# A cross-attention and Strassen feed-forward kernel: the first keys on another queue, the first normalisation reordered, and small work moved between units

## The chip, the cores and the metric

One core of a Trainium2 chip runs the whole program. The metric is the device time of one execution in microseconds; lower is better. The engines are TensorE (PE, with its weight loads PEld), VectorE (DVE), ScalarE (ACT), GpSimd (POOL) and SyncE (SP), which only issues transfers. ScalarE and GpSimd issue transfers too. Each engine runs its own instructions strictly in the order in which the program emitted them.

## The reference

The input is `x` (8 x 256 x 256), a context of the same shape and a key mask. Each row of `x` is normalised over its 256 values and attends, causally, to the context, which is keys and values at once; the result is added to `x`. The sum is normalised again and goes through a feed-forward network with ternary weights, each with a scale for every output; its result is added once more:

```
x = x + softmax(mask(layernorm(x) @ ctx.T / 16)) @ ctx
y = layernorm(x)
h = silu((y @ w1.T) * s1) * ((y @ w2.T) * s2)     # 256 -> 1024
h = gelu((h @ h1.T) * t1)                         # 1024 -> 1024
h = gelu((h @ h2.T) * t2)                         # 1024 -> 1024
out = x + (h @ w3.T) * s3                         # 1024 -> 256
```

## The kernel before, in words

The 2048 tokens are four blocks `t` = 0 to 3 of 512 tokens (two batches `j`). The blocks run in two pairs `s`: pair 0 holds blocks 0 and 1, pair 1 blocks 2 and 3. A pair's two blocks go through the two 1024 x 1024 products together, as a Strassen scheme with seven products of halves of 512; a block's hidden values are in halves `a` and `b` (first block) and `c` and `d` (second block), and sums such as `T1 = c - a` and `T2 = d - T1` are operands. Every operand is split into a rounded part `oh` (a cast on ScalarE, `parted`) and a rest `ol` (a subtraction on VectorE, `rest`, L313), and both are multiplied.

**Units and the plan.** `pair(s, ...)` is a generator; what it emits between two `yield`s is a unit, and each pair has 80. Units 0 to 7 are the gated first layer of the pair's first block (`pa`, `pb`, then SiLU `gate` on ScalarE L697 and a product with it on VectorE L700). For the first hidden layer follow: product 1 (8 to 11), product 2, called `second`, whose four results `p` are added to `na` by VectorE L855 (12 to 15), the gated layer of the second block with the making of T1 and T2 (16 to 23), and products 6, 5, 3, 7, 4 (24 to 43). The second hidden layer runs products 1, 6, 5, 3, 7, `second`, 4 (44 to 71), and units 72 to 79 are the output layer (`po`, `res` L711). Most units take TensorE 1.81 us. After each unit the actions that the table `plan` names for it are emitted, so the numbers in `stages_at`, `looks` and `at` decide where in each engine's queue the small work stands.

**Stages.** The attention of a block (`stages`) is a chain of such actions. For blocks 2 and 3 the queries come from memory; late in the chain `sums` takes the statistics of the new `x`, `on_all` turns mean and reciprocal deviation over (TensorE `tmf` L393, a copy, and a path through memory), L659 and L660 normalise on VectorE and GpSimd, `casts` (ScalarE L606) and `rests` (VectorE L313) make `hyt` and `lyt`, the operands of the gated layer, and the transfer `kept` stores the transposed `x` for the end.

**Head.** Block 0 is split into two groups, one batch each, that advance in turn stage by stage, so that each engine has the other group's work between two steps of one. For each group: `sums` (L261, L262), `normed` (square root L269 on ScalarE, reciprocal L275, `scaled` L283 on VectorE, giving `ya`), `turned` (TensorE `pqt`), a scaled copy to `qt`, scores `ps`, softmax, `pv`, the add to `x` (L551), and the second normalisation. Group 0's second normalisation is taken by ScalarE from sums, and its finish (`begun`) lies in the list `held`, from which `sums` of group 1 takes it. Five warm-up matmuls stand on TensorE's queue between `pxt` and `pyt` of group 1. All loads of block 0 but the mask are issued by SP: four tiles of `x`, then the keys `kt` of group 0 and of group 1, then `vs`.

**Looks.** `look_through` tests 22 pieces of the weights in turn: six small ones, each with one VectorE reduce (`seen`, L212), and 16 wide ones, each with a sign pass on ScalarE (L216) and a comparing pass on VectorE (L218). One call issues the load of piece k (`raw`, 512 KB, three buffers, on SP), finishes with L218 the piece signed by the call before, and signs or reduces piece k - 2. A call's load waits for the buffer that its own L218 frees. Twenty-five calls are needed.

Of the kernel before, what the change touches and what calls it, by code (L numbers as in the profile page):

```python
# [43 lines left out]
P = 128  # L44
B, S, D, H = 8, 256, 256, 1024
NB = 2
NT = NB * S // P
# [27 lines left out]
def _network(ctx, tc, g, exact, flag):  # L75
# [23 lines left out]
    def groups(t):  # L99

        return ((0,), (1,)) if t == 0 else ((0, 1),)
# [4 lines left out]
    def tiles(js):  # L106
        return slice(2 * js[0], 2 * js[-1] + 2)

    def load_block(t, behind=None):

        xs = new(io, [P, NT, D], "xs", f"xs_{t}", bufs=2)
        kt = new(io, [P, NB, ND, S], "kt", f"kt_{t}", bufs=2)
        vs = new(io, [P, NT, D], "vs", f"vs_{t}", bufs=2)
        mi = new(io, [P if t else 1, TB], "mi", f"mi_{t}", I32)
        span = bass.ts(t, TB)
        if behind is not None:
            for tile_ in (xs[:, 0, :1], kt[:, 0, 0, :1], vs[:, 0, :1], mi[:, :1]):
                behind.memset(tile_, 0)
        if t == 0:
            nc.scalar.dma_start(out=mi, in_=g.mask[:, span])  # L120
        step = NT if t else 1
        for i in range(0, NT, step):
            nc.sync.dma_start(out=xs[:, i : i + step, :], in_=g.x[t, :, i : i + step, :])
        for n, js in enumerate(groups(t)):
            own = slice(js[0], js[-1] + 1)
            nc.sync.dma_start(out=kt[:, own], in_=g.ctx_t[t, :, own])
            if n == 0 and t:
                nc.sync.dma_start(out=mi, in_=g.mask[:, span].to_broadcast([P, TB]))
        nc.sync.dma_start(out=vs, in_=g.ctx_n[t])
        return xs, kt, vs, mi  # L130
# [123 lines left out]
        yield  # L254
        yield nc.values_load(flag[0:1, 0:1], min_val=0, max_val=P * (LOW + len(wide) * RAW))

    def sums(src, js, mv, name, between=()):

        stats = new(tiny, [P, NT, nc.vector.BN_STATS_DIM], "stats", f"st{name}", bufs=2)
        for i in range(NT)[tiles(js)]:  # L260
            nc.vector.bn_stats(out=stats[:, i, :], in_=src[:, i, :])  # L261
            nc.vector.bn_aggr(out=mv[:, :, i], in_=stats[:, i, :])  # L262
            while between:
                between.pop()()

    def root(js, mv, name):
        own = tiles(js)
# [10 lines left out]
    def normed(src, js, mv, y, name):  # L278
        scaled(src, range(NT)[tiles(js)], mv, turned_over(js, root(js, mv, name), name), y)
# [32 lines left out]
    def rest(lo, value, hi):  # L312
        nc.vector.tensor_tensor(lo, value, hi.bitcast(F32), ALU.subtract)  # L313
# [91 lines left out]
    def queries_turned(t, js, once, xs, mi, pss):  # L405

        cols = tokens(js)
        mva = once("mva", "mva", [P, nc.vector.BN_AGGR_DIM, NT], tiny, bufs=2)
        sums(xs, js, mva, f"a_{t}_{js[0]}")
        if t == 0 and js == groups(t)[0]:  # L410
            nc.vector.tensor_scalar(row16[:, :TB], mi, 0.0, NEG, ALU.is_equal, ALU.mult)
        if not t:
            masks_first(js, pss)
        yield
        y = once("y", "ya", [P, NT, D])
        normed(xs, js, mva, y, f"a_{t}_{js[0]}")
        if t == 0 and js == groups(t)[-1]:
            passed = new(const, [P, 1], "passed", "passed")
            nc.gpsimd.tensor_copy(passed, y[:, NT - 1, :1])
        yield  # L420
        bias = mask_bias(t, js, once, mi)
        qt = once("qt", "qt", [P, ND, TB])
        for c, pt in turned(y, js, f"pqt_{t}_{js[0]}", *(() if t else (ps_mm, "mm"))):

            if t or js == groups(t)[0]:
                nc.scalar.activation(qt[:, c, cols], pt, AF.Copy, scale=1.0 / 16.0)
            else:
                nc.vector.tensor_scalar(qt[:, c, cols], pt, 1.0 / 16.0, None, ALU.mult)
        table(t, js, AF.Exp)
        yield  # L430
        return qt, bias, None
# [25 lines left out]
    def stages(t, js, once, result, xs, kt, vs, mi):  # L457
# [68 lines left out]
        for j in js:  # L526
            if t:
                pv = ps_at.tile([P, 2, D], F32, tag="at", name=f"{v}pv_{t}_{j}")
                pvs = [pv[:, h, :] for h in range(2)]
            else:  # L530

                p, tag = (ps_at, "at") if j else (ps_mm, "mm")
                pvs = [p.tile([P, D], F32, tag=tag, name=f"{v}pv_0_{j}_{h}") for h in range(2)]
            for h, (a, e) in enumerate(SPANS):
                n = (e - a) // P
                for k in range(n):
                    nc.tensor.matmul(  # L537
                        pvs[h],
                        lhsT=prt[:, j, bass.ds(a + k * P, P)],
                        rhs=vs[:, 2 * j + k, :],  # L540
                        start=(k == 0),
                        stop=(k == n - 1),
                    )

            first_ = len(groups(t)) > 1 and js == groups(t)[0]
            if first_:
                total, centre, squares, std = (
                    new(const, [P, 2], n, n) for n in ("total", "centre", "squares", "std0")
                )
            for h in range(2):  # L550
                nc.vector.scalar_tensor_tensor(  # L551
                    xs[:, 2 * j + h, :],
                    pvs[h],
                    rden[:, j, h : h + 1],
                    xs[:, 2 * j + h, :],
                    ALU.mult,
                    ALU.add,
                    **(dict(accum_out=total[:, h : h + 1]) if first_ else {}),
                )
        if t:  # L560
            yield
        mvf = once("mvf", "mvf", [P, nc.vector.BN_AGGR_DIM, NT], tiny)
        if first_:
            y = once("y", "yf", [P, NT, D])
            for i in range(2):
                nc.scalar.activation(
                    centre[:, i : i + 1], total[:, i : i + 1], AF.Copy, scale=-1.0 / D
                )
                nc.scalar.activation(
                    y[:, i, :],  # L570
                    xs[:, i, :],
                    AF.Square,
                    bias=centre[:, i : i + 1],
                    accum_out=squares[:, i : i + 1],
                )
            nc.scalar.activation(std, squares, AF.Sqrt, bias=eps, scale=1.0 / D)

            def begun():

                nc.vector.reciprocal(std, std)  # L580
                shifted(0, nc.gpsimd)

            def shifted(i, engine):
                engine.tensor_scalar(
                    y[:, i, :],
                    xs[:, i, :],
                    centre[:, i : i + 1],
                    std[:, i : i + 1],
                    ALU.add,
                    ALU.mult,  # L590
                )

            held.append(begun)
        else:
            sums(xs, js, mvf, f"f_{t}_{js[0]}", held)
        yield
        xst = once("xst", "xst", [P, ND, TB])
        yt = []
# [13 lines left out]
        def rests(values):  # L612
            for c, value in values if not exact else ():
                rest(yt[1][:, c, cols], value, yt[0][:, c, cols])

        def turned_x():
            pxt = turned(xs, js, f"pxt_{t}_{js[0]}")
# [8 lines left out]
        if near(t):  # L626
# [16 lines left out]
            if not t and not first_:  # L643
                residual_turned(pxt)
            yield
            rests(values)
        else:
            std = once("sq", "sdf", [P, NT], tiny, bufs=2)
            nc.scalar.activation(std, mvf[:, 1, :], AF.Sqrt, bias=eps)
# [12 lines left out]
            values = [(slice(c, c + 1), y[:, c : c + 1, :]) for c in range(ND)]  # L662
            casts(values)
            yield
            rests(values)
        if js == groups(t)[-1]:
            nc.sync.dma_start(out=kept(t), in_=xst)
        result[:] = yt
# [124 lines left out]
    def half(tag, name):  # L793

        return new(hp, [P, 2, TB], tag, name, bufs=2)
# [37 lines left out]
    def pair(s, places, stock):  # L833
# [74 lines left out]
        for n in (2, 3):  # L908
# [64 lines left out]
            if first_:  # L973
# [4 lines left out]
                for o in range(NH):  # L978
# [10 lines left out]
                    )  # L989
                    if not s and o in (2, 4):  # L990
                        fetch(o // 2 + 1)
                    if o in (2, 4):
                        T1[o // 2 - 1] = half(place["T1"], f"T1_{name}_{o}")
                        sub(T1[o // 2 - 1], c[o // 2 - 1], a[o // 2 - 1])

                    if o == 5:
                        T2[:] = [half(place["T2"], f"T2_{name}_{h}") for h in range(2)]
                        sub(T2[0], d[0], T1[0])
                    if o == 6:
                        X[6] = parted(T2[:1], f"{name}_6")  # L1000
                        rest(X[6][0][1], T2[0], X[6][0][0])
                        sub(T2[1][:, 0, :], d[1][:, 0, :], T1[1][:, 0, :])
# [165 lines left out]
    def sums_from(r):  # L1168
# [5 lines left out]

    stages_at(1, (0, 0), (0, (1, 2, 4, 5, 7, 9, 10, 10, 10, 11, 13, 14)))
    stages_at(
        2, (0, 8), (0, (25, 28, 30, 41, 45, 46, 49, 51, 53, 54, 55, 57, 58, 61, 62, 63))
    )
    stages_at(
        3, (0, 30), (0, (55, 56, 59, 70, 73, 74, 75, 77, 78, 79)), (1, (0, 1, 5, 8, 10, 13))  # L1180
    )
    at(0, (7, 7, 14, 15), lambda: next(summing[2], None))
    at(0, 9, lambda: sums_from(0))
# [1 line left out]
    at(0, 21, lambda: sums_from(1))  # L1185
    at(0, (32, 33, 34, 37), lambda: next(summing[4], None))
    at(0, 44, lambda: w3.extend(load_weight(g.w3t, "w3_")))
    at(0, (72, 74, 76, 78), lambda: next(looking, None))
    looks = (1, 3, 5, 8, 10, 12, 14, 16, 17, 19, 26, 27, 42, 44, 46, 47, 50, 51, 54, 55, 58)
    at(1, looks, lambda: next(looking, None))  # L1190
    at(1, 61, lambda: [None for _ in looking])
    at(1, (66, 70), lambda: next(ending))
# [65 lines left out]
```

## Time and profile before

| | us |
|---|---|
| median of three runs | 349.14 |
| lowest and highest | 347.75, 349.73 |
| the profiled execution, its own time | 347.43 |
| its span, first to last instruction | 345.6 |
| TensorE, VectorE, ScalarE, GpSimd busy | 334.0, 270.3, 216.4, 36.6 |

The clock that TensorE was granted was 0.995 of full speed. Times in the lines below are microseconds from the start of the span. A line of the timeline gives start, time, engine, source line, operation, output and inputs, their shapes and the number of instructions, and in brackets how long the engine had been idle and what ended that. A matmul's end is modelled and overlaps the next one, so lost time is read from the starts.

### The profile page before, as it was taken

The numbers are of one execution on the slowest core, as the hardware profiler recorded it, in microseconds if no ns is written. First come the engines' busy times: TensorE is split into PE (matmuls) and PEld (weight loads), VectorE is DVE, ScalarE is ACT, GpSimd is POOL, SyncE is SP. The second block draws the span as 40 slices with busy tenths as digits, with TensorE's granted clock in tenths as the row PEclk, the third lists the DMA queues.
The fourth block names the chain that finished last, engine by engine and source line by source line (L and its number), as shares of the span: only waits on it lengthen the run. The fifth ranks groups of instructions, "written<-read, shape, count | busy, mean of one in ns | idle before, by whom it ended". The sixth has DMA issues, their size and how long they took to land.

```text
span 345.6 us, 4329 instructions
## 1 busy us (share of the span) xinstructions
PE 334.0 (97%) x1508; PEld 269.9 (78%) x1508; DVE 270.3 (78%) x411; ACT 216.4 (63%) x301; POOL 36.6 (11%) x78
## 2 busy tenths in 40 slices
PE   8999999999999999999999999999999999999991
PEld 4777887877888888887888788886788887888781
DVE  5779876999799848686997875889948987856761
ACT  4866833358855854858671675356896686767620
POOL 3610000210002300030000003000010000000000
PEclk9999999999999999999999999999999999999998
DMA  5999972997596642579517474960635579530032
GB/s 184 342 297 273 294 256 82 358 280 252 151 399 228 197 146 99 164 251 326 204 47 246 127 251 127 292 248 2 243 123 182 173 250 353 201 121 0 0 123 70
DMA packets 20702, 68.81 MB, mean 199 GB/s; under 512 B 2465, under 2 KB 5313, under 8 KB 17090
## 3 DMA queue, kind: packets, MB, share of 16 engines
q0 software_dynamic: 7488, 36.70, 33.0%
q1 hardware_dynamic: 13040, 31.63, 27.2%
q8 instruction: 14, 0.23, 0.3%
q14 instruction: 14, 0.11, 0.1%
q10 hardware_dynamic: 146, 0.13, 0.1%
HBM read 55.86 MB, written 8.40 MB: 186 GB/s over the span
## 4 chain that ended last, share of the span: by engine, by line
PE 79%; DVE 8%; DMA 5%; ACT 3%; issue 2%; POOL 1%; DVEq 0%; POOLq 0%; ACTq 0%; SPq 0%
PE px_u L824 29%; PE px_y L824 15%; PE po L1112 8%; PE p L824 7%; PE pa L684 5%; PE pb L684 5%; PE ps L470 3%; PE pv L537 3%; DMA raw<-h2q 3%; DMA raw<-h1q 1%; DVE sign L218 1%; DVE ol L313 1%; PE pqt L301 1%; ACT oh L807 1%; DVE sta L261 1%
## 5 line engine op out<-in xcount | busy, mean ns | idle before, releaser
L824 PE MATMUL px_u<-oh,a 128*128 128x512 f32 x256 | 71.7, 395 | 1.1 <-ACT oh L807 0.8
L824 PE MATMUL px_u<-ol,a 128*128 128x512 f32 x256 | 70.8, 391 | 0.0
L824 PEld LDWEIGHTS px_u<-ol,a 128*128 128x128 f32 x256 | 47.9, 188 | 11.6 <-DVE ol L313 1.5
L824 PEld LDWEIGHTS px_u<-oh,a 128*128 128x128 f32 x256 | 47.5, 188 | 11.8 <-ACT oh L807 1.2
L697 ACT ACTIVATE gate<-pa,sc 128x512 f32<-128x512 f32 x32 | 21.6, 686 | 24.5 <-PE pa L684 22.1
L824 PE MATMUL px_y<-oh,a 128*128 128x512 f32 x128 | 34.5, 391 | 0.0
L824 PE MATMUL px_y<-ol,a 128*128 128x512 f32 x128 | 34.2, 389 | 0.0
L824 PEld LDWEIGHTS px_y<-ol,a 128*128 128x128 f32 x128 | 24.0, 188 | 5.0
L824 PEld LDWEIGHTS px_y<-oh,a 128*128 128x128 f32 x128 | 23.9, 188 | 5.0
L216 ACT ACTIVATE sign<-raw 128x1024 bf16<-128x1024 f32 x16 | 16.9, 1055 | 9.5 <-DMA raw<-h2q 4.1
L768 POOL DMA_DIRECT2D a<-S x16 | 8.5, 534 | 131.6 <-PE px_u L824 55.5
L218 DVE SCALAR_TENSOR_TENSOR sign<-raw,sign 128x1024 bf16<-128x1024 f32 x16 | 19.3, 1219 | 2.7 <-ACT sign L216 2.7
L684 PE MATMUL pa<-hyt,w 128*128 128x512 f32 x60 | 19.1, 399 | 0.2 <-DVE na L855 0.2
L684 PE MATMUL pb<-hyt,w 128*128 128x512 f32 x60 | 18.6, 391 | 0.2 <-DVE res L711 0.2
L684 PE MATMUL pa<-lyt,w 128*128 128x512 f32 x60 | 18.5, 390 | 0.0
L684 PE MATMUL pb<-lyt,w 128*128 128x512 f32 x60 | 18.5, 389 | 0.0
L852 ACT ACTIVATE nd<-nd,sc 128x512 f32<-128x512 f32 x16 | 10.7, 715 | 11.7 <-DVE nd L855 11.7
L824 PE MATMUL p<-oh,a 128*128 128x512 f32 x64 | 17.4, 394 | 0.4 <-DVE na L855 0.4
L313 DVE TENSOR_TENSOR ol<-nT,oh 128x1024 fp32r<-128x1024 f32 x12 | 14.5, 1222 | 3.6 <-ACT oh L807 3.6
L824 PE MATMUL p<-ol,a 128*128 128x512 f32 x64 | 17.1, 389 | 0.0
L855 DVE TENSOR_TENSOR na<-p,na 128x512 f32<-128x512 f32 x16 | 10.9, 688 | 7.9 <-PE p L824 7.9
L852 ACT ACTIVATE nb<-nb,sc 128x512 f32<-128x512 f32 x16 | 10.7, 717 | 10.0 <-DVE nb L855 10.0
(196 smaller groups left out, 651.1 us busy)
## 6 DMA issues: line engine op xcount, KB each, us to landing
a<-S POOLq DMA_DIRECT2D x16, 1024.0 KB, 5.1
a<-h1q POOLq DMA_DIRECT2D x6, 1024.0 KB, 7.8
a<-h2q POOLq DMA_DIRECT2D x6, 1024.0 KB, 5.1
raw<-h1q SPq DMA_DIRECT2D x8, 512.0 KB, 4.3
raw<-h2q SPq DMA_DIRECT2D x8, 512.0 KB, 5.9
vs<-ctx_n SPq DMA_DIRECT2D x4, 512.0 KB, 7.5
q<-h1q POOLq DMA_DIRECT2D x4, 512.0 KB, 20.1
q<-h2q POOLq DMA_DIRECT2D x8, 256.0 KB, 14.0
```

Source lines behind the costliest of these rows:

```text
L216: nc.scalar.activation(sign, raw, AF.Sign)
L218: nc.vector.scalar_tensor_tensor(sign, raw, 1.0, sign, ALU.mult, ALU.not_equal, accum_out=count[:, n : n + 1])
L313: nc.vector.tensor_tensor(lo, value, hi.bitcast(F32), ALU.subtract)
L470: nc.tensor.matmul(pss[j][h], lhsT=qt[:, c, bass.ts(2 * j + h, P)], rhs=kt[:, j, c, : e - a], start=(c == 0 and t > 0), stop=(c == ND - 1) ...
L537: nc.tensor.matmul(pvs[h], lhsT=prt[:, j, bass.ds(a + k * P, P)], rhs=vs[:, 2 * j + k, :], start=(k == 0), stop=(k == n - 1),)
L684: nc.tensor.matmul(pm, lhsT=wc[:, bass.ts(o, P)], rhs=x, start=(n == 0), stop=(n == len(steps) - 1),)
L697: nc.scalar.activation(gate, pa, AF.Silu, scale=sc[:, 0, o : o + 1])
L768: nc.gpsimd.dma_start(out=a, in_=src)
L824: nc.tensor.matmul(bank, lhsT=a[:, k, bass.ts(o, P)], rhs=x[k // 2][part][:, k % 2, :], start=start and (part, k) == steps[0], stop=stop a ...
L852: nc.scalar.activation(out, src, AF.Gelu, scale=sc[:, n, o : o + 1])
L855: nc.vector.tensor_tensor(out, one, other, ALU.add)
L1112: nc.tensor.matmul(po, lhsT=w3[j * QK + k][:, bass.ts(o, P)], rhs=xs_[j][k // 2][part][:, k % 2, :], start=(j == 0 and (part, k) == STEPS[0]),
```

## The change

1. **Keys.** The first group's keys are issued on ScalarE's queue instead of SP's.
2. **First normalisation.** Group 0's square root, reciprocal and scaling (its tile 0 on GpSimd) are put into `held` and emitted between the two tiles of group 1's `sums`.
3. **Adds.** In block 0's group 1, `sums` emits each tile's add (L551) just ahead of that tile's statistics (`ahead`), and `held` is taken before the second tile instead of after the first.
4. **T1.** In pair 1 the second half of T1 is made in unit 21 behind T2's first half, instead of in unit 20.
5. **Block 2's rests** become three actions, in units 68, 69 and 69 (and with them `kept`), instead of one in unit 63. Block 3's are split the same way but stay in unit 13 of pair 1.
6. **Looks.** In pair 0 the four calls come two units earlier. In pair 1 the calls at 17 and 19 become one at 18, and those at 50 and 51 move to 51 and 52; the last call is made by the clearing action of unit 61.
7. **Statistics turned.** Block 3's `on_all` moves from unit 1 to unit 2 of pair 1.

```diff
-            nc.sync.dma_start(out=kt[:, own], in_=g.ctx_t[t, :, own])
+            queue = nc.sync if t or n else nc.scalar
+            queue.dma_start(out=kt[:, own], in_=g.ctx_t[t, :, own])
...
-    def sums(src, js, mv, name, between=()):
+    def sums(src, js, mv, name, between=(), ahead=None):
-        for i in range(NT)[tiles(js)]:
+        for n, i in enumerate(range(NT)[tiles(js)]):
+            if ahead is not None:
+                ahead(n)
+            while n and between:
+                between.pop()()
             nc.vector.bn_stats(out=stats[:, i, :], in_=src[:, i, :])
             nc.vector.bn_aggr(out=mv[:, :, i], in_=stats[:, i, :])
-            while between:
-                between.pop()()
...
-        sums(xs, js, mva, f"a_{t}_{js[0]}")
-        if t == 0 and js == groups(t)[0]:
+        sums(xs, js, mva, f"a_{t}_{js[0]}", held)
+        y = once("y", "ya", [P, NT, D])
+        very_first = t == 0 and js == groups(t)[0]
+        if very_first:
+            def begun():
+                rstd = turned_over(js, root(js, mva, "a_0_0"), "a_0_0")
+                scaled(xs, (0,), mva, rstd, y, nc.gpsimd)
+                scaled(xs, (1,), mva, rstd, y)
+            held.append(begun)
...
-        normed(xs, js, mva, y, f"a_{t}_{js[0]}")
+        if not very_first:
+            normed(xs, js, mva, y, f"a_{t}_{js[0]}")
...
-            for h in range(2):
+            def added(h, j=j, pvs=pvs):
...
+            if t or first_:
+                added(0)
+                added(1)
...
-            sums(xs, js, mvf, f"f_{t}_{js[0]}", held)
+            sums(xs, js, mvf, f"f_{t}_{js[0]}", held, None if t else added)
...
                 rest(yt[1][:, c, cols], value, yt[0][:, c, cols])
+                yield
...
-            rests(values)
+            yield from rests(values)
...
-                    if o in (2, 4):
-                        T1[o // 2 - 1] = half(place["T1"], f"T1_{name}_{o}")
-                        sub(T1[o // 2 - 1], c[o // 2 - 1], a[o // 2 - 1])
+                    if o == 2:
+                        T1[:] = [half(place["T1"], f"T1_{name}_{h}") for h in range(2)]
+                        sub(T1[0], c[0], a[0])
+                    if o == 4 and not s:
+                        sub(T1[1], c[1], a[1])
                     if o == 5:
                         T2[:] = [half(place["T2"], f"T2_{name}_{h}") for h in range(2)]
                         sub(T2[0], d[0], T1[0])
+                    if o == 5 and s:
+                        sub(T1[1], c[1], a[1])
...
-        2, (0, 8), (0, (25, 28, 30, 41, 45, 46, 49, 51, 53, 54, 55, 57, 58, 61, 62, 63))
+        2, (0, 8), (0, (25, 28, 30, 41, 45, 46, 49, 51, 53, 54, 55, 57, 58, 61, 62, 68, 69, 69))
...
-        3, (0, 30), (0, (55, 56, 59, 70, 73, 74, 75, 77, 78, 79)), (1, (0, 1, 5, 8, 10, 13))
+        3, (0, 30), (0, (55, 56, 59, 70, 73, 74, 75, 77, 78, 79)), (1, (0, 2, 5, 8, 10, 13, 13, 13))
...
-    at(0, (72, 74, 76, 78), lambda: next(looking, None))
-    looks = (1, 3, 5, 8, 10, 12, 14, 16, 17, 19, 26, 27, 42, 44, 46, 47, 50, 51, 54, 55, 58)
+    at(0, (70, 72, 74, 76), lambda: next(looking, None))
+    looks = (1, 3, 5, 8, 10, 12, 14, 16, 18, 26, 27, 42, 44, 46, 47, 51, 52, 54, 55, 58)
```

More of the change, by code (lines that the diff above doesn't have):

```diff
@@ L414, in queries_turned @@
         yield
-        y = once("y", "ya", [P, NT, D])
-        normed(xs, js, mva, y, f"a_{t}_{js[0]}")
+        if not very_first:
+            normed(xs, js, mva, y, f"a_{t}_{js[0]}")
         if t == 0 and js == groups(t)[-1]:
@@ L645, in stages @@
             yield
-            rests(values)
+            list(rests(values))
         else:
@@ L664, in stages @@
             yield
-            rests(values)
+            yield from rests(values)
         if js == groups(t)[-1]:
```

## The prediction

> **What bounds the kernel now.** I read the page's busy table first:
>
> ```profile
> PE 334.0 (97%) x1508; PEld 269.9 (78%) x1508; DVE 270.3 (78%) x411; ACT 216.4 (63%) x301; POOL 36.6 (11%) x78
> ```
>
> TensorE (PE) sets the time; nothing in the change touches its work, so only its waits and the head before its steady stream (from 18.69 us) count. Next I read TensorE's timeline for holes. Four 512-column matmuls start every 0.91 us, 0.227 each; whatever exceeds that is lost.
>
> ```profile
> 155.76 1.07 PE L824 MATMUL p<-ol,a 128*128 128x512 f32 x4
> 157.27 0.50 PE L824 MATMUL p<-oh,a 128*128 128x512 f32 x1 [0.43 <-DVE na L855]
> ...
> 191.02 0.61 PE L684 MATMUL pa<-lyt,w 128*128 128x512 f32 x2
> 191.83 0.73 PE L684 MATMUL pb<-hyt,w 128*128 128x512 f32 x2 [0.20 <-DVE res L711]
> 192.40 0.62 PE L684 MATMUL pb<-lyt,w 128*128 128x512 f32 x2
> 193.27 0.27 PE L393 MATMUL tmf<-ident,mvf 128*8 128x128 f32 x1 [0.25 <-DVE mvf L651]
> ...
> 233.77 0.61 PE L684 MATMUL pb<-lyt,w 128*128 128x512 f32 x2
> 235.16 0.50 PE L824 MATMUL px_u<-oh,a 128*128 128x512 f32 x1 [0.77 <-ACT oh L807]
> ...
> 289.35 1.07 PE L824 MATMUL px_u<-ol,a 128*128 128x512 f32 x4
> 290.72 0.50 PE L824 MATMUL px_u<-oh,a 128*128 128x512 f32 x1 [0.30 <-ACT nb L943]
> ```
>
> From the starts: 156.67 was due and 157.27 came, 0.60 lost; then 0.36 and 0.42; 234.23 due, 235.16 came, 0.93; 290.26 due, 290.72 came, 0.46. Each restart loses about another 0.11 (after 157.27 the next group of four starts 1.03 later, not 0.91). The change moves VectorE (DVE) and ScalarE (ACT) work at exactly these places. Both engines run in program order, so what I read third is what queues behind what. ScalarE at the last hole, the loads of `raw`, and ScalarE just behind:
>
> ```profile
> 288.70 1.06 ACT L216 ACTIVATE sign<-raw 128x1024 bf16<-128x1024 f32 x1 [2.77 <-DMA raw<-h2q]
> 289.67 1.00 ACT L943 COPY nb<-px_u 128x1024 f32<-128x1024 f32 x1
> ...
> 297.71 1.99 ACT L807 CAST oh<-nc 128x1024 fp32r<-128x1024 f32 x2
> 299.60 1.25 ACT L852 ACTIVATE nc<-px_u,sc 128x512 f32<-128x512 f32 x2
> ```
> ```profile
> DMA to landing us min/median/max: 3.7/5.3/9.2
> ```
>
> A sign pass stood 2.77 us for a 512 KB load, and the copy that TensorE needed stood behind it. Last, VectorE in the head:
>
> ```profile
> 4.57 0.41 DVE L261 BATCH_NORM_STATS2 sta<-xs 128x6 f32<-128x256 f32 x1
> ...
> 5.54 0.18 DVE L262 BATCH_NORM_AGGREGATE mva<-sta 128x2 f32<-128x6 f32 x1
> ...
> 6.66 0.74 DVE L283 TENSOR_SCALAR ya<-xs,mva,rsa 128x256 f32<-128x256 f32 x2
> ```
>
> The second `ya` pair ends at 7.40, the last transposes follow, and the scores start at 7.84.
>
> **The change, part by part** (clock: the profiled execution, 347.43 us, span 345.64).
>
> *Rests of block 2, unit 63 to 68/69.* Today they run at 154.67 and 155.92, waiting on GpSimd and the casts, and hold `na` (L855) to 156.53. Without them `na` of unit 64 runs at 155.1 and the 0.60 goes. What is late next: `ol<-nT`, released when `oh` ends at 156.83, then the second `na` at 158.0 + 0.69 = 158.69, while TensorE wants its bank at 158.49: about 0.26 comes back. Net -0.34. Their new place, 166 to 169, has VectorE full (two rests, 1.25 us); what comes after them is the score pass at 173.44, and the queue in front of it then ends at 173.3. SP's `kept` write waits for nothing there: nought.
>
> *Looks two units earlier in pair 0, statistics turned at unit 2.* The first three `raw` loads leave earlier and nobody waits for them. The second `seen` reduce (1.19, at 189.93) now stands before `res` L711 (191.03); `res` follows the statistics at 189.93 and the 0.36 goes. Moving `seen` up costs VectorE 1.2 us between 178.9 and 186.6, where its next TensorE-bound step (`res` at 187.13) has room. TensorE's `tmf` then no longer waits in front of a reciprocal that is queued behind a gate. Of 0.97 with restarts I keep 0.85, since `pa` of unit 2 needs the first gate, done at 192.34, and is due at 192.38.
>
> *T1 second half behind T2, one look fewer among the gates (pair 1, units 16 to 23).* Between 222 and 234 VectorE runs three `sign` passes (1.15 each) and T1 twice (1.14). One of each leaves the path to T2: T2 starts with its gate at 231.65 rather than 232.80, `oh` ends at 233.95, and the 0.93 goes. Next late is T2's second half: T1's half, `ol`, `hd` and the one-row rests bring the last operand at 239.2, where TensorE would want it by 238.55. Today that unit ends at 240.13, then at 239.60: -0.53.
>
> *Looks from units 50, 51 to 51, 52.* The copy `nb` no longer stands behind a waiting sign: -0.57 (0.46 + 0.11). But all looks from there on are now one piece late. Follow the load issued at unit 52. The `sign` pass of VectorE that frees its buffer is emitted behind that unit's rests. ScalarE: sign 288.70 (its load landed at 288.62), `oh` from 289.67, so the first rest starts at 290.70; two rests take 2.35, the pass 1.22: 294.2. SP issues at 294.3, and unit 55 asks for the sign of that piece. Before, this load left at 287.67, 6.6 us ahead of its sign. ScalarE stands until it has landed (L after issue); then sign 0.96, two `oh` 1.89, two `gelu` 1.32: 4.2 us until `gelu` has emptied the bank that unit 60 writes. Unit 60 is due at 290.26 + 6 x 1.8145 = 301.15. Wait = 294.3 + 0.1 + L + 4.2 + 0.1 - 301.15 = L - 2.5. No load in the trace is under 3.7: the wait is at least 1.1. Rows by their neighbours: 4.7 (issued 219.9 to 221 with a 1 MB fetch just behind), 5.9 (287.67, a fetch 0.6 ahead), 9.2 (279.39, another load and a fetch around it). Here a fetch goes out at unit 56, 294.35, the same moment. I take the median 5.3: 2.75 + 0.11 = 2.85. Ends: 1.3 at 3.7 and 6.8 at 9.2. A later stand of the pass at unit 61 (309.1 at the latest before today's `nd` at 309.3) is covered.
>
> [...]
>
> *Head.* Group 0's normalisation now sits between the third and the fourth statistics. VectorE: aggregate 5.02, reciprocal 5.12, `ya` tile 1 at 5.29, statistics 5.62, aggregate 6.04; then square root, reciprocal and `ya` take what they take at 16.35 to 17.83 (1.48): 7.52 instead of 7.40, +0.13, because ScalarE's square root is no longer hidden under group 0's work. Group 0 itself, with tile 0 on GpSimd (0.55, as its like at 16.19), is ready 0.3 earlier, but TensorE transposes group 1 before the scores.
> The keys of group 0 aren't awaited: issued at 2.59, a landing 3.7 later is 6.3, used from 7.84. What they do is share the transfers: 256 KB enter while the four `x` tiles arrive, each needed within 0.2 to 0.6 us of landing. DMA is 0.75 to 0.77 busy at 2.5 to 4.5, so between 0 and 0.5 us; I take 0.25, for the spare quarter is less than what the keys ask. The second interleaving (statistics between the two adds) pulls the aggregate 0.28 forward but frees the `pxt` bank 0.2 later, and the warm-up matmuls behind it hold the transposes: nought, -0.1 to +0.1. The weights' loads on GpSimd's queue follow the last `ya` and shift with it; the last lands at 18.1 and is first used at 19.3. Head: +0.38, 0 to 0.8.
>
> [...]
>
> Sum: -0.34 - 0.85 - 0.53 - 0.57 + 2.85 + 0.38 = +0.94: 348.4 for the profiled execution. That one is 1.7 under the median of the runs, so on the median it is 350.1.
>
> **Rivals.** *Forecast, within 0.5%* (1.75 us, about what a measurement of this kernel can tell from no change): L from 3.7 to 6.1, so -0.6 to +1.75.
> *Slower, one mechanism:* the load issued at 294.3 is caught between the fetch at 294.35 and the next load (295.4), as at 279.39. At L = 9.2 unit 60 waits 6.8, the sum is +4.9: 354. It decides from L = 6.1 up. For: two neighbours compete; against: it is first in its queue.
> *Faster:* the load lands at 3.7 (1.3), the four holes close in full (0.71 + 0.97 + 1.04 + 0.57 = 3.29) and the head costs nothing: -2.0, 347.1. Against: three lucky ends at once.
> *The holes only move:* VectorE is full where the rests go; if scores slip by their 1.25, +2.2, 351.3. Against: the score chain has 1.5 us before its transposes at 178.35.
>
> **How the numbers follow.** Forecast 0.58; slower 0.34 (long load 0.2, moved holes and head at its end 0.14); faster 0.08. Range: 347.5 (short of the faster case) to 353.4 (L about 8.6), leaving about a tenth at each end. The likeliest case alone: 348.5 to 350.9.
>
> **What would show it.** Holes at 156.7, 191.5, 234.2 and 290.3 gone or shrunk to 0.3, none, 0.7 (spread), none. A new hole in `px_y` ahead of unit 60, released by `gelu` L852, with a sign waiting for `raw<-h2q` before it. Scores in the head after 7.84. Wrong if that sign doesn't wait, or if the first scores start earlier than now.

## The result and the profile after

The changed kernel takes 349.07 us (median of 22 runs, 347.31 to 350.38) against 347.61 before (22 runs, 345.73 to 349.73): a ratio of 1.0055, 95% interval 1.0039 to 1.0071. It is a little slower, at the edge between the forecast ("within 0.5%", 350.1) and the slower case, and inside the range. The forecast was counted from 349.14, the median of three runs of the kernel before; over 22 runs that kernel takes 347.61. So 349.07 lies 1.0 under the forecast time, while the change itself is larger than forecast: +1.46 between the medians and 0.55% (1.9 us) by the ratio, against +0.94. In a later comparison the same kernel came to 1.0076 (1.0052 to 1.0100). The profiled execution took 348.98, span 347.2; that of before 347.43 and 345.64.

TensorE's busy time is the same as before:

```profile
PE 334.3 (96%) x1507; PEld 271.3 (78%) x1508; DVE 268.8 (77%) x410; ACT 216.8 (62%) x301; POOL 38.1 (11%) x79
```

TensorE's timeline at the holes that the prediction followed, with the start of the steady stream ahead of them (columns: start, duration, engine, line, operation, and in brackets the idle time and who ended it):

```profile
21.13 0.78 PE L911 MATMUL pa<-hyt,w 128*128 128x512 f32 x2 [0.39 <-ACT hyt L630]
...
160.09 1.07 PE L845 MATMUL p<-ol,a 128*128 128x512 f32 x4
161.26 1.20 PE L845 MATMUL p<-oh,a 128*128 128x512 f32 x4
...
194.09 0.61 PE L705 MATMUL pb<-lyt,w 128*128 128x512 f32 x2
194.90 0.74 PE L705 MATMUL pa<-hyt,w 128*128 128x512 f32 x2 [0.19 <-ACT gate L718]
...
239.68 0.39 PE L845 MATMUL px_u<-oh,a 128*128 128x512 f32 x1
240.24 0.50 PE L845 MATMUL px_u<-ol,a 128*128 128x512 f32 x1 [0.17 <-DVE ol L318]
...
301.45 1.07 PE L845 MATMUL px_u<-ol,a 128*128 128x512 f32 x4
303.42 0.96 PE L845 MATMUL px_y<-oh,a 128*128 128x512 f32 x3 [0.90 <-ACT nc L873]
```

From the starts, each with its restart of 0.11: 0.27 is lost at 161, 0.35 at 194.6, 0.33 at 240 (and 0.22 once more at 240.8), nothing at 290, and 1.06 ahead of 303.42 (302.36 was due). Against the profile of before that is a gain nearly everywhere, but the steady stream starts at 21.13 instead of 18.69. ScalarE ahead of the last hole shows the wait that the prediction named, a sign on a load:

```profile
299.26 1.06 ACT L218 ACTIVATE sign<-raw 128x1024 bf16<-128x1024 f32 x1 [2.37 <-DMA raw<-h2q]
300.22 1.98 ACT L828 CAST oh<-nc 128x1024 fp32r<-128x1024 f32 x2
302.11 1.25 ACT L873 ACTIVATE nc<-px_u,sc 128x512 f32<-128x512 f32 x2
```

The head is what came out differently. TensorE there:

```profile
1.18 3.59 PE L163 MATMUL warm<-zeros 128*128 128x512 bf16 x9 [1.18 <-DVE zeros L166]
4.60 0.22 PE L375 MATMUL ps<-masks 128*128 128x128 bf16 x1
5.86 0.21 PE L382 MATMUL ps<-row 1*128 1x128 bf16 x1 [1.04 <-DVE row L426]
...
7.93 1.97 PE L306 MATMUL pqt<-ident,ya 128*128 128x128 f32 x8 [0.69 <-POOL ya L288]
9.73 3.49 PE L485 MATMUL ps<-kt,qt 128*128 128x128 f32 x16
```

The scores start at 9.73 (the forecast said only: after 7.84). Two stands are new, 1.04 us for the row of the masks and 0.69 us for GpSimd's tile, and the 16 scores take 3.49 us where they took 2.89 before. The third fact explains the last: the granted clock, read by stretches (columns: stretch, length, busy time and count of PE, PEld, DVE, ACT, POOL, then PE's clock, DMA share, GB/s). After:

```profile
4.30:7.70 3.40, 1.90 (x11) 0.75 (x8) 2.40 (x9) 0.55 (x2) 1.18 (x1) 0.99 0.94 296
7.70:11.10 3.40, 3.17 (x13) 2.91 (x14) 1.70 (x5) 2.03 (x4) 2.50 (x6) 0.51 0.20 64
11.10:14.50 3.40, 2.77 (x17) 2.28 (x16) 2.09 (x7) 2.23 (x10) 3.10 (x11) 1.00 1.09 347
```

and before, where TensorE was busy for 3.27 of the same 3.40 us and kept its clock to 11.1 and beyond:

```profile
4.30:7.70 3.40, 3.27 (x18) 1.59 (x16) 2.95 (x12) 1.10 (x3) 0.24 (x2) 1.00 0.83 285
```

So for 3.4 us after the stretch with the two stands TensorE ran at half speed. Where the first stand comes from is told by the `x` tiles, in the summary of that tile's loads (issue to landing). Before, it reads 2.4 at least and at most; after:

```profile
DMA to landing us min/median/max: 2.4/3.7/4.0
```

The 3.7 is tile 1's. VectorE's statistics of that tile and its row for the masks, which stands behind them, before and then after:

```profile
3.74 0.39 DVE L261 BATCH_NORM_STATS2 sta<-xs 128x6 f32<-128x256 f32 x1
...
4.26 0.38 DVE L411 TENSOR_SCALAR row<-mi 1x512 bf16<-1x512 int32 x1
```
```profile
4.87 0.43 DVE L268 BATCH_NORM_STATS2 sta<-xs 128x6 f32<-128x256 f32 x1 [1.05 <-DMA xs<-x]
...
5.43 0.38 DVE L426 TENSOR_SCALAR row<-mi 1x512 bf16<-1x512 int32 x1
```

### The profile page after: what moved, and what is told of

Read it like the earlier page. It is cut to its first block, busy times and chain, and to the rows that moved or that the text cites. A ratio compares the mean times of both kernels' runs of the same rounds, so it can differ in the third digit from the quotient of the medians.

```text
span 347.2 us, 4330 instructions
## 1 busy us (share of the span) xinstructions
PE 334.3 (96%) x1507; PEld 271.3 (78%) x1508; DVE 268.8 (77%) x410; ACT 216.8 (62%) x301; POOL 38.1 (11%) x79
## 4 chain that ended last, share of the span: by engine, by line
PE 71%; DVE 12%; DMA 5%; ACT 4%; issue 4%; POOL 1%; SPq 0%; DVEq 0%; POOLq 0%; ACTq 0%
PE px_u L845 24%; PE px_y L845 15%; PE p L845 6%; PE pa L705 6%; PE pb L705 6%; PE po L1139 5%; PE ps L485 3%; DMA raw<-h2q 2%; DVE ol L318 2%; PE pv L552 2%; DMA res<-kept 2%; ACT oh L828 2%; PE pqt L306 1%; DMA xs<-x 1%; DVE T L879 1%
## 5 line engine op out<-in xcount | busy, mean ns | idle before, releaser
L718 ACT ACTIVATE gate<-pa,sc 128x512 f32<-128x512 f32 x32 | 21.8, 688 | 27.7 <-PE pa L705 25.1
```

What stands on the lines that cost most here:

```text
L718: nc.scalar.activation(gate, pa, AF.Silu, scale=sc[:, 0, o : o + 1])
```

## Experiments

Spans differ by up to 1.1 us behind TensorE's last matmuls (last `po` to the end: 6.3 to 7.4 us, whatever the kernel), so beside the times I compare stretches of the profiles, all read from starts in TensorE's timeline: the head (to the first `pa` of the steady stream), pair 0 (from there to the first `po`) and pair 1 (from the last `po` of pair 0 to the first `po` of pair 1). The two `po` stretches are 20.23 and 14.29 in every profile. Ratios are against the kernel before timed in the same comparison, with their 95% intervals. "Keys" are the first group's keys; where nothing else is said, an edit is made on the changed kernel.

| kernel | ratio | head | pair 0 | pair 1 |
|---|---|---|---|---|
| before, profile of the prediction | | 18.69 | 149.61 | 135.46 |
| before, again | 1.0005 (0.9983 to 1.0027) | 18.68 | 149.67 | 134.34 |
| changed | 1.0055 (1.0039 to 1.0071) | 21.13 | 149.33 | 134.99 |
| changed, again | 1.0076 (1.0052 to 1.0100) | 22.01 | 149.35 | 135.04 |
| keys back | 1.0013 (0.9992 to 1.0034) | 18.90 | 149.29 | 134.43 |
| normalisation back | 1.0059 (1.0038 to 1.0079) | 21.06 | 149.31 | 134.69 |
| both back | 1.0030 (1.0010 to 1.0051) | 21.83 | 149.29 | 133.98 |
| more warm-ups | 1.0048 (1.0030 to 1.0067) | 20.21 | 149.29 | 135.38 |
| keys alone, on before | 1.0054 (1.0029 to 1.0078) | 22.37 | 149.73 | 134.36 |
| keys later | 1.0026 (1.0006 to 1.0046) | 20.36 | 149.37 | 135.04 |
| keys back, signs moved | 0.9990 (0.9967 to 1.0012) | 18.87 | 149.38 | 133.52 |
| keys back, looks at 50, 51 | 0.9971 (0.9949 to 0.9993) | 20.44 | 149.32 | 133.47 |
| both back, signs moved | 0.9968 (0.9948 to 0.9989) | 18.77 | 149.31 | 134.64 |
| the same, 11 warm-ups | 0.9985 (0.9966 to 1.0004) | 18.61 | 149.33 | 134.36 |

**Keys back.** Theory A was that the keys' transfer delays the second `x` tile and TensorE's idle time then halves its clock; rival B, that GpSimd's tile is to blame.

```diff
-            queue = nc.sync if t or n else nc.scalar
+            queue = nc.sync
```

> The changed kernel with the first keys on SyncE's queue again. Theory A (the keys' transfer delays x tile 1, so that VectorE's row for the masks comes a microsecond late, TensorE stands idle and its clock drops to half): x tile 1 lands at 3.6 again, the mask matmuls run through to 6.2, the clock stays at 1.00, the steady stream starts at 18.8 to 19.0 and the kernel is 2.2 us faster than the changed one, 0.7 us faster than the one before (-0.2%). Rival B (GpSimd's 1.36 us tile is what leaves TensorE idle): TensorE still stands before the first pqt, the clock drops, the stream starts at 20 or later and no more than 1.2 us comes back.

Tile 1 landed at 3.55, the stream started at 18.90 with the clock at 1.00, and the kernel is level with before. A holds for the head: with GpSimd's tile still there (1.36 us) 2.23 us came back. The hoped-for lead over before didn't come; the profiles of before below say why.

**Normalisation back.**

```diff
-        very_first = t == 0 and js == groups(t)[0]
+        very_first = False
...
             held.append(begun)
+        if t == 0 and js == groups(t)[0]:
             nc.vector.tensor_scalar(row16[:, :TB], mi, 0.0, NEG, ALU.is_equal, ALU.mult)
```

> The changed kernel with the first group's normalisation in its old place (after the fourth statistics, both tiles on VectorE); the keys stay on ScalarE's queue. Theory A: x tile 1 still lands at 4.8, the row still comes at 5.4, TensorE still stands 1.0 us among the mask matmuls; the stream starts between 19.9 (clock kept, since the second stand in front of pqt shrinks from 0.69 to 0.2) and 20.6 (clock halved): 0.5 to 1.2 us faster than the changed kernel, still slower than before the change. Rival B: the stream starts by 19.2, 1.9 us or more come back.

Nothing came back: 1.0059, stream at 21.06. B falls. But A's wording falls too. TensorE stood only 0.16 for the row (its warm-ups had ended 0.4 later) and 0.19 for the first `pqt`, and the clock halved all the same, from 8.6 to 12.0:

```profile
5.20:8.60 3.40, 2.98 (x17) 1.55 (x15) 2.82 (x11) 1.17 (x4) 0.37 (x2) 1.00 0.63 205
8.60:12.00 3.40, 3.40 (x14) 3.03 (x13) 1.41 (x3) 1.92 (x4) 3.39 (x11) 0.50 0.70 222
```

Again the half-clock stretch is 3.4 us long, and it lies elsewhere than in the changed kernel (7.6 to 11.0). The clock's own entries in the changed kernel's trace read 3.413 us full, 3.413 half and 334.506 full, 98 times the 3.413; the trace of before has one full-clock stretch of 337.919, 99 times it. So the length of a single stand doesn't decide (1.04 and 0.69 in one profile, 0.16 and 0.19 in the other); what does isn't shown.

**Both back.** The two edits above together.

> The changed kernel with both edits of the head undone (keys on SyncE's queue, first normalisation in its old place); the rest of the change stays. If the changed kernel's steady part is worth what its trace shows, -0.9 us from the stream's start on, the stream starts at 18.7 and the kernel is 0.9 us faster than before, 2.3 us faster than the changed one. If the steady part is worth nothing and the trace misleads, it equals the kernel before within 0.3 us.

Neither answer. Steady part as hoped (pair 0 149.29, pair 1 133.98), but the head took 21.83: TensorE's timeline shows it at half speed from the first instruction on.

```profile
1.19 4.02 PE L163 MATMUL warm<-zeros 128*128 128x512 bf16 x9 [1.19 <-DVE zeros L166]
...
8.99 4.92 PE L486 MATMUL ps<-kt,qt 128*128 128x128 f32 x16
```

The 16 scores take 4.92 us instead of 2.89, and the 256-column mask matmuls 0.33 from start to start instead of 0.22. Every profile starts so: the warm-ups of 512 columns come every 0.427 us and, once the clock is full, every 0.216. In nine of the 14 profiles the clock was full from a time between 3.8 and 5.7 us; in five (this one, the changed kernel again, the keys alone, the keys later, the looks at 50, 51) only from 10.2 to 13.5. The clock column reads 1.00 all the while, so the spacing of the matmuls is what must be read. The head is code for code that of "both back, signs moved", which started its stream at 18.77 with the clock full early: the late full clock costs 3 us here and isn't the edit's. What makes a start late isn't shown. My estimate counts back from the moment of full clock in lengths of the 3.413 us of the entries: the nine early profiles then have one length with at least 2.65 us of warm-up matmuls in it, and in the five late ones the warm-ups fall across two, with at most 2.36 in either. There are no entries that far ahead to bear the lengths out, and no run moves it deliberately. The 12 times show the two kinds too, five from 345.2 to 346.2 and seven from 347.4 to 348.4.

**More warm-ups.** Six matmuls on zeros in the idle time of the changed kernel.

```diff
+            if very_first:
+                keep_warm(4)
             masks_first(js, pss)
+            if not very_first:
+                keep_warm(2)
```

> The changed kernel with six more warm-up matmuls on zeros, four ahead of the first mask matmul and two behind the last: they fill TensorE's idle time before the first pqt and do nothing else. If it is the idle time that halves TensorE's clock from 8 to 11 us, the clock stays at 1.00, the scores take 2.9 instead of 3.5 us, and the stream starts 1.0 to 1.4 us earlier (about 19.9): that much faster than the changed kernel. If the clock drops for another reason, or if the half clock is hidden behind VectorE and ScalarE, nothing changes (within 0.3 us).

```profile
8.13 1.04 PE L306 MATMUL pqt<-ident,ya 128*128 128x128 f32 x8
9.41 2.89 PE L489 MATMUL ps<-kt,qt 128*128 128x128 f32 x16 [0.25 <-ACT qt L445]
...
20.21 0.79 PE L915 MATMUL pa<-hyt,w 128*128 128x512 f32 x2 [0.39 <-ACT hyt L634]
```

Transposes 1.04 instead of 1.97, scores 2.89 instead of 3.49, stream 0.92 earlier: so much was the half clock in this pair of profiles. The times don't decide it: 1.0048 against the changed kernel's 1.0055 and 1.0076, where 0.3 to 0.4% less was expected. In this profile 0.60 is lost ahead of unit 60 and another 0.93 at 306, behind a sign that stood 2.47 for its load, and pair 1 takes 135.38. What stays of the head, 20.21 against 18.69, is 1.52 of lateness; 0.21 of it is there without the early keys (18.90), so the keys' own delay is 1.3 us.

**Before and changed, again**, both kernels as they are, on one chip.

> The kernel before, unchanged, on the chip of the three others and with a second profile. If the profile that the prediction was made from is typical, its holes stand again: 0.60 at 156.7, 0.36 and 0.42 at 191 to 193, 0.93 at 234.2, 0.46 at 290.3, the stream starts at 18.7, and the ratio to itself is 1.000 within 0.002. If the holes that a load's landing makes vary from run to run, the one at 290 is shorter or gone.

> The changed kernel, unchanged, on the same chip: ratio 1.004 to 1.007. Theory of the clock (TensorE's clock is decided at fixed steps of about 3.4 us that do not start with the program): the spans of its runs fall into groups by their mean clock, about half of them with 0.989 to 0.990 as one 3.4 us step at half clock makes it (1.7 us in 347), and the profile may show the half-clock stretch elsewhere between 5 and 13 us. Rival (the clock drops because of this kernel's idle times alone, at the same place each time): the stretch at half clock is again 7.7 to 10.9.

The second profile of before has the holes at 156.7 (0.60) and 191 to 193 (0.36, 0.41), but only 0.57 at 234 and none at 290:

```profile
234.83 1.42 PE L824 MATMUL px_u<-oh,a 128*128 128x512 f32 x5 [0.41 <-ACT oh L807]
...
289.02 1.07 PE L824 MATMUL px_u<-ol,a 128*128 128x512 f32 x4
289.92 1.07 PE L824 MATMUL px_u<-oh,a 128*128 128x512 f32 x4
```

The profile with the keys alone, whose steady part is that of before, agrees (0.57, none). The prediction's profile was the odd one by 1.1 us in pair 1, so 0.9 of what the change was to win there is mostly not there to be won. The second profile of the changed kernel is one of those with a late full clock (13.1 us), so it can't show where a drop to half clock would lie; against the rival of a fixed place speaks only the normalisation back (8.6 to 12.0). Its two pairs take what they took in the first profile within 0.05.

The mean clocks of the timed runs separate the kernels (3.4 us at half speed lower the mean over 347 by 0.005): 0.991 or less stands in 31 of 53 runs with early keys and no added warm-ups (the changed kernel in both comparisons, the normalisation back, the keys alone), in 0 of 6 with them, and in 2 of 190 of all others, the runs of before among them.

**Keys alone**, on the kernel before.

```diff
-            nc.sync.dma_start(out=kt[:, own], in_=g.ctx_t[t, :, own])
+            queue = nc.sync if t or n else nc.scalar
+            queue.dma_start(out=kt[:, own], in_=g.ctx_t[t, :, own])
```

> The kernel before with the first keys on ScalarE's queue and nothing else. Theory A (the keys are what costs): x tile 1 lands at 4.8, not 3.6; VectorE's head is 1.0 to 1.1 us later, the stream starts at 19.7 with a full clock and at 21 with a halved one; 1.0 to 2.4 us slower than before (1.003 to 1.007). Theory of the prediction (0.25 us of shared transfers): 1.001, within 0.3 us of before.

1.0054: this one edit makes as much as the whole change. VectorE started on tile 1 at 4.89, after standing 1.07 for it. The stream at 22.37 holds a late full clock as well.

**Keys later**: on ScalarE's queue, but behind its table load and first square root, issued at 3.16.

```diff
-            queue = nc.sync if t or n else nc.scalar
+            queue = nc.sync
+            if not (t or n):
+                later_keys.append((kt, own))
+                continue
             queue.dma_start(out=kt[:, own], in_=g.ctx_t[t, :, own])
...
     nc.scalar.activation(junk, eps, AF.Sqrt)
+    for kt_, own_ in later_keys:
+        nc.scalar.dma_start(out=kt_[:, own_], in_=g.ctx_t[0, :, own_])
```

> The changed kernel with the first keys still on ScalarE's queue, but issued behind its table load and first square root, at 2.8 instead of 1.3 us. If it is the time of the issue that costs (256 KB beside tiles that are still on their way), x tile 1 lands at 3.6 again, no run shows a mean clock of 0.988 to 0.991, the stream starts at 18.9 where the clock is full, and it equals the run with the keys back on SyncE's queue (1.000 to 1.002). If the second queue itself slows SyncE's transfers, tile 1 still lands after 4.4 and the kernel stays 1.005 or more.

Tile 1 landed at 3.58, and the summary of the `x` loads is that of before, 2.4 at least and at most. One of 12 mean clocks is under 0.991. So it isn't the queue that costs, but the moment. The time, 1.0026, is a little above what was expected; its profile has a late full clock and 1.45 lost ahead of unit 60.

**Signs moved**: keys back, and the last two looks behind the gelus that free the banks.

```diff
-    looks = (..., 47, 51, 52, 54, 55, 58)
+    looks = (..., 47, 51, 52, 54, 57, 59)
```

> The changed kernel with the first keys on SyncE's queue, and the looks of pair 1 at units 55 and 58 moved to 57 and 59, behind the gelus that free TensorE's banks. If the waiting sign is what holds unit 60, the hole ahead of px_y of unit 60 (0.71 in the run with the keys alone back) is gone and the end comes 0.6 to 0.8 us earlier than there: 345.6 where the kernel before takes 346.1 (0.998). If unit 60 waits for something else, the hole stays or moves to unit 62 or 64 and nothing is gained (1.001).

```profile
298.97 1.07 PE L845 MATMUL px_u<-ol,a 128*128 128x512 f32 x4
299.88 1.07 PE L845 MATMUL px_y<-oh,a 128*128 128x512 f32 x4
```

The hole ahead of unit 60 is gone, pair 1 takes 133.52. The time, 0.9990, doesn't tell this from no gain; the stretch does.

**Looks at 50 and 51, and the mean added on GpSimd**, with the keys back.

```diff
-    looks = (..., 47, 51, 52, 54, 55, 58)
+    looks = (..., 47, 50, 51, 54, 55, 58)
-                scaled(xs, (0,), mva, rstd, y, nc.gpsimd)
+                nc.gpsimd.tensor_scalar(... ALU.add, ALU.mult)
```

> The changed kernel with the first keys on SyncE's queue and two more edits that are read in different stretches. (1) The looks of pair 1 stand at units 50 and 51 again, not 51 and 52. Theory (each look now handles a piece whose load left one look earlier, so neither the sign of unit 51 nor that of unit 55 has to wait): no hole at 290 and none ahead of unit 60, pair 1 takes 133.5 as in the run with the signs moved. Rival (the shift to 52 is what closes the hole at 290): the hole of 0.46 stands there again. (2) In the first group's tile on GpSimd the mean is added instead of subtracted (the values of that tile are other ones; its size and operands are the same): if the operation makes the difference between 1.36 and 0.55 us, it takes 0.55 and the first pqt comes at 6.6; if not, 1.36 again.

ScalarE in pair 1:

```profile
288.66 1.06 ACT L218 ACTIVATE sign<-raw 128x1024 bf16<-128x1024 f32 x1 [0.44 <-DMA raw<-h2q]
...
293.17 1.06 ACT L218 ACTIVATE sign<-raw 128x1024 bf16<-128x1024 f32 x1 [0.65 <-DMA raw<-h2q]
...
295.25 1.06 ACT L218 ACTIVATE sign<-raw 128x1024 bf16<-128x1024 f32 x1
```

The signs ahead of unit 60 wait 0.44 and 0.65, where ScalarE has room; a later one, at 301.50, waits 2.15 and costs TensorE nothing. Neither hole is there, pair 1 takes 133.47, and the kernel is a little faster than before: 0.9971 (0.9949 to 0.9993). So in this profile, with one look fewer ahead of them, 50 and 51 were good places, and the step to 52 only bought the wait at unit 60. GpSimd's tile with subtract (the changed kernel; 1.36 too at 5.35 with the keys back), then with add:

```profile
6.52 1.36 POOL L288 TENSOR_SCALAR ya<-xs,mva,rsa 128x256 f32<-128x256 f32 x1 [3.64 <-DVE rsa L280]
```
```profile
5.37 0.68 POOL L422 TENSOR_SCALAR ya<-xs,mva,rsa 128x256 f32<-128x256 f32 x1 [2.50 <-DVE rsa L280]
```

Half the time. That this brings `pqt` forward couldn't be seen, since the masks ran at half clock here.

**Both back, signs moved**, and **the same with 11 warm-ups**, made of edits shown above and this one for the second.

```diff
-WARM, WARM_LATER = 9, 5
+WARM, WARM_LATER = 11, 5
```

> The steady part of the change without its first two edits, and with the two looks at 57 and 59: first keys on SyncE's queue, first normalisation in its old place. Where the clock is full early, the stream starts at 18.6, pair 0 takes 149.35 and pair 1 133.5: 1.2 us under the kernel before (0.9965). Where TensorE stays at half clock from the start, as in the profile with both edits of the head undone, the stream starts at 21.8. If the gains of the steady part are lost again at the end, 1.000.

> The same with 11 warm-up matmuls on zeros at the start instead of 9. TensorE has about 0.7 us of waits among its first transposes, so two more (0.43) should cost 0 to 0.3 us where the clock is full. If a step of 3.4 us with too little work is what leaves the clock at half, a busy stretch longer by 0.43 to 0.85 makes such starts rarer: fewer runs 2.5 to 3 us above the lowest. If the number of slow starts has nothing to do with it, the share stays and the median is 0 to 0.3 us above the run before it.

The first is faster than before by 0.3% (0.9968) and, by way of before, than the changed kernel. Pair 1 isn't at its best, though: with the last sign at unit 59 its load landed only at 303.02, 9.95 us after issue, and what stands behind that sign (from 303.11) costs 1.02 at 311.

Two more warm-ups settle nothing: the times are close together in both (344.7 to 347.0, 344.8 to 346.6), and neither falls into two groups as those of "both back" do. The head of this kernel with the looks at 50 and 51 would be the next to try; it wasn't run.

## Why the prediction was right, and where it was not

The number held by luck: errors of opposite sign met, and the median that it was counted from was 1.5 us high. Term by term, read from how much later than before the same matmul starts at the two ends of each stretch (the terms come to +1.70, the difference of the last `po`, 338.27 before and 339.97 after; against the second profile of before to +2.76):

| term | predicted | measured | against before, again |
|---|---|---|---|
| rests of block 2 | -0.34 | -0.34 | -0.35 |
| statistics, looks earlier | -0.85 | -0.39 | -0.37 |
| T1, one look fewer | -0.53 | -0.56 | -0.20 |
| looks 51, 52: hole at 290 | -0.57 | -0.73 | 0 |
| wait at unit 60, to the end | +2.85 | +1.21 | +1.21 |
| head | +0.38 | +2.44 | +2.45 |
| units of pair 0 ahead of the rests | 0 | +0.07 | +0.02 |

**The rests** went as worked out: 0.71 gone, 0.27 + 0.11 back at unit 67, and pair 0 is 149.29 to 149.38 in all profiles that have the edit, 149.61 to 149.73 in those that don't. Nothing slipped behind the score pass, so "the holes only move" falls.

**The statistics**: the mechanism was right, with the gate (L718) as what is late next, but one cost was put at nothing ("nobody waits for them"). The earlier look puts a `seen` reduce between two `res` of the output layer (181.02), so the loads `res<-kept` that follow on SP's queue leave 0.8 later against their units (183.31, before 180.31), and the first `res` that needs one stood for it. Before, then after:

```profile
187.13 0.75 DVE L711 SCALAR_TENSOR_TENSOR res<-po,s,res 128x512 f32<-128x512 f32 x1 [0.97 <-PE po L1112]
```
```profile
189.63 0.75 DVE L732 SCALAR_TENSOR_TENSOR res<-po,s,res 128x512 f32<-128x512 f32 x1 [1.05 <-DMA res<-kept]
```

The statistics and the gate behind it are 0.33 late by that. The gain is 0.39 here and 0.59 and 0.65 in the two other profiles in which this `res` waits for the load; in the eight in which it waits for TensorE, as before, it is 0.66 to 0.74. So -0.85 was never reached.

**T1** hit its size, 1.31 to 0.77 of lost time, the spread of 0.7 included, but from a hole of 0.93 that is 0.57 in the two other profiles of the old code.

**The hole at 290** is gone, as forecast, with 0.16 of smaller delays behind it; the failing step is its price: one profile had shown it, two others of the same code don't.

**Unit 60**: right mechanism, right chain (from the landing at 299.18 to TensorE at 303.42 are 4.24 us; 4.2 and 0.1 were worked out), wrong size. The step that failed is "I take the median 5.3": the load that leaves first in its queue landed after 3.9 to 4.4 in all ten profiles with this order. It also left 0.6 earlier against unit 60 than worked out, since that unit was due 1.2 later than in the prediction's clock and the load only 0.7. (Its own sum for a landing after 5.3 gives 2.85 ahead of the restart, not 2.75.) The slower rival named the catch of a load by a fetch and a neighbour; this happens to the load 1.1 us behind it, whose sign starts 8.0 to 9.95 us after the issue in those profiles and which has more room.

**The head** is the step that was most wrong, 2.44 against 0.38 and outside its own bounds (0 to 0.8): "I take 0.25, for the spare quarter is less than what the keys ask". A mean busy share of the transfers over two microseconds doesn't say when one tile lands. With 256 KB issued 0.1 us after it, tile 1 took longer: 2.4 us became 3.3 to 3.7, tile 1 came 0.9 to 1.3 later, and since VectorE's row for the masks stands behind its statistics, TensorE's whole head moved by 1.3. Two smaller steps: GpSimd's tile was priced at 0.55 "as its like", which adds where this one subtracts (1.36), with a cost of only 0.2 as long as the masks still run (18.90 against 18.68, +0.13 forecast); the second interleaving is nought, as said. And one was missing: the clock. The prediction counted idle time of TensorE in the head at its own length; here a half-clock stretch of 3.4 us followed it, worth 0.92 in the pair of profiles without and with more warm-ups.

What makes the clock drop stays open. Stands of 1.04 and 0.69 us within one stretch of 3.4 (the changed kernel) were followed by half clock, and so were stands of 0.16 and 0.19 with short matmuls between (the normalisation back); a stretch with TensorE busy for 2.98 of 3.40 lost the clock, one with 2.77 (11.10 to 14.50 in the changed kernel) didn't. The price of the keys no row of before showed; the keys alone and the keys later do: issued 0.1 us after tile 1, from another queue, they bring it in about 1 us late (VectorE starts on it at 4.89 in the keys alone, at 3.74 before), and issued at 3.16 they don't (it lands at 3.58).

## What to carry to other kernels

Don't issue a large load that is needed late beside small ones that are needed first: 256 KB of keys, issued from another queue 0.1 us after a 128 KB tile, made that tile land after 3.3 to 3.7 us instead of 2.4; issued at 3.16 they didn't. Ahead of the steady stream, price a stand of TensorE by what its clock does afterwards as well (0.92 us here), and read the spacing of equal matmuls, not the clock row alone. Take a hole that hangs on a load's landing from two or three profiles before its removal is entered as a gain.

## What the hardware showed unexpectedly

- TensorE's clock was at half for one stretch of 3.4 us in the head, from 7.6 to 11.0 in the changed kernel's first profile and from 8.6 to 12.0 with the normalisation back.
- At the start it is half speed (512 columns every 0.427 us) until 3.8 to 5.7 us in nine profiles and until 10.2 to 13.5 in five; the clock column shows 1.00 there. The late head is 1.5 us longer where this lasts to 10.2 (20.36 against 18.90; the two differ in the keys' late issue) and 3.1 where it lasts to 13.2 (21.83 against 18.77, equal code).
- GpSimd takes 1.36 us for a 128x256 subtract-and-multiply and 0.68 for the same tile with add (one run).
- Of two 512 KB loads 1.1 us apart with another engine's fetch between, the first landed after 3.9 to 4.4 us, and the sign that waited for the second started 8.0 to 9.95 us after its issue (ten profiles).
